# Cross-attention in fp32 on one core: seven products for three more batches, sums from ScalarE, roots from logarithms

## The chip, the core and the metric

The kernel runs on one core of a Trainium2 chip. A core has five engines that run side by side, each through its own queue in order: PE (TensorE, matmuls; its weight loads are shown apart as PEld), DVE (VectorE), ACT (ScalarE), POOL (GpSimd) and SP (SyncE, which issues DMAs here). They wait for each other through semaphores. The metric is the device time of the program in microseconds (us), the median of some runs.

## The reference

```python
Q = (img_embed @ Wq).reshape(B, -1, H, D).transpose(0, 2, 1, 3)
K = (sent_embed @ Wk).reshape(B, -1, H, D).transpose(0, 2, 1, 3)
V = (sent_embed @ Wv).reshape(B, -1, H, D).transpose(0, 2, 1, 3)
score = jnp.einsum('bhqd,bhkd->bhqk', Q, K) / math.sqrt(D)
score = jnp.where(mask, score, -jnp.inf)
attn = jax.nn.softmax(score, axis=-1)
ctx = jnp.einsum('bhqk,bhkd->bqhd', attn, V).reshape(B, -1, H * D)
out = ctx @ Wo + img_embed
mu = jnp.mean(out, axis=-1, keepdims=True)
var = jnp.var(out, axis=-1, keepdims=True)
return (out - mu) * jax.lax.rsqrt(var + EPS) * gamma + beta
```

There are 16 batches of 256 rows of `img_embed` (256 wide) and 77 rows of `sent_embed` (192 wide), 8 heads with D = 256. All is fp32.

## The kernel before

**Setup.** The weights are multiplied with each other first: `gA`, `gB` hold Wk and Wq of each head in one product, `uA`, `uB` hold Wv and Wo of each head in one product. A batch then needs three contractions: `a` (context times `gA`, `gB`), the scores `ps` (x times `a`), and the output `po` (softmax weights times `vw`, where `vw` is context times `uA`, `uB`).

**Tiles and groups.** A tile is 128 rows of x, so a batch has two tiles and there are 32. Four batches are a group: `xT` and `a` are made for a whole group ahead, one quarter in each batch of the group before. The last group (batches 12 to 15) has no group after it, so while its batches are scored PE has no `a` to make.

**The loop.** The order of the work is written out by hand in one loop over b from -1 to 14. A turn of the loop handles three batches at once: `new` are the tiles of batch b + 1 (scores, exponentials, weights), `now` those of batch b (output contraction), `old` those of batch b - 1 (layer norm, stored). Every engine takes its instructions in the order in which the turn names them:

- `scores` (PE, L311), `shift` (DVE: scores from PSUM plus the mask's bias, L326; the negated maximum of each head, L333);
- `prepare_vw` and `prepare_a` (PE, L239 and L250, L197 and L211); their results leave PSUM by copies on ACT (L884);
- `exponential` (ACT, L340, one instruction a head with that head's maximum as bias), `weigh` (DVE: the sum of each head over its 77 keys, L346, and its reciprocal, L348; POOL: the multiplication into `p`, two instructions at L354);
- `finish` (DVE: statistics of the layer norm, L482 and L485), `spread` (ACT: square root, L493), `invert` (DVE: reciprocal, L500), `normalise` (DVE: `centre`, L514, then L530; with `aside` ACT L524 and POOL L525, L526 instead, for which `invert` makes `less`, L504), then the store, a DMA that SP issues for each batch once both tiles are done;
- `turn` (DVE: transposes p in 32 x 32 blocks to `pT`, L364), `transpose_x` (DVE, L173, two in each of the last two batches of a group);
- for `now`, either `attend` or `seven`.

`attend` (L376) is the direct form: for each of the two tiles, five weight blocks against 256 columns. `seven` (L427) takes the two tiles, the two halves of the keys and the two halves of the columns as 2 x 2 blocks and forms them with seven block products instead of eight (the Strassen-Winograd scheme), plus the products of the last 13 keys. It needs the differences of `vw`'s parts (`differences`, POOL, L390, into `ts`), four sums of the weights (`sums`, POOL, L407 to L410, into `ss`), made a turn ahead, and after the products an ACT copy of four of them (`m`, L450) and `add_seven`: two additions of `po` on DVE (L474) and five additions on POOL (L460). `NS` is the number of batches that are done so: 11 before, batches 0 to 10. `prepare_vw` lays out `vw` for one form or the other.

**Tables.** ACT's functions come in sets of tables, of which one is loaded at a time. Exp and Sqrt stand in different ones in this program, so each turn loads two (the rows ACT_TABLE_LOAD at L493 and at L890 or L911). The tiny activation `warm` (L890, L911) makes the load for Exp happen before the exponentials are due.

**Buffers.** PSUM's eight banks are one ring, `ps_mm`: a new tile waits until the reader of the tile eight places before it is done. `s`, `e`, `p`, `ts`, `ss` are double buffered, `m` is single.

**The end.** After the loop the last batch is contracted with `attend`, and the last four tiles are finished and normalised one after the other, with DVE, ACT and POOL sharing the work.

Of the kernel before, what the change touches and what calls it, by code (L numbers as in the profile page):

```python
# [8 lines left out]
F32 = mybir.dt.float32  # L9
I32 = mybir.dt.int32  # L10
AF = mybir.ActivationFunctionType
# [4 lines left out]
P = 128  # L16
H = 8
# [36 lines left out]
def kernel(  # L54
# [53 lines left out]
    NH = DI // 2 // BK  # L108
    uA = const.tile([P, 5, NH, NF, BK], F32, tag="uA", name="uA")
    uB = const.tile([P, 5, NH, NF, BK], F32, tag="uB", name="uB")  # L110
    NS = B - GB - 1

    def of_e(u, e):
        return u[:, 3 - 2 * e : 5 - 2 * e].rearrange("p q n i c -> p (q n) i c")
# [218 lines left out]
        nc.vector.tensor_reduce(top, s, AX.X, ALU.max, negate=True)  # L333
        s_of[t] = s, top

    def exponential(t):
        e = sp.tile([P, H, S2], F32, tag="e", name=f"e_{t}")
        s, top = s_of.pop(t)
        for h in range(H):
            nc.scalar.activation(e[:, h], s[:, h], AF.Exp, bias=top[:, h : h + 1])  # L340
        e_of[t] = e

    def weigh(t):
        e = e_of.pop(t)
        den = st.tile([P, H], F32, tag="den", name=f"den_{t}")
        nc.vector.tensor_reduce(den, e, AX.X, ALU.add)  # L346
        rden = st.tile([P, H], F32, tag="rden", name=f"rden_{t}")
        nc.vector.reciprocal(rden, den)  # L348
        p = p_ring[t % 2]
        e_mh = e.rearrange("p (m h) k -> p m h k", h=2)  # L350
        rden_mh = rden.rearrange("p (m h) -> p m h", h=2)
        for cols, keys in ((slice(2 * KM), slice(KM)), (slice(2 * KM, 2 * S2), slice(KM, None))):
            part = p[:, :, cols].rearrange("p m (h k) -> p m h k", h=2)
            nc.gpsimd.tensor_tensor(  # L354
                part,
                e_mh[:, :, :, keys],
                rden_mh.unsqueeze(3).to_broadcast(list(part.shape)),
                ALU.mult,
            )

    def turn(t):
        p = p_ring[t % 2]
        pT_of[t] = turned.tile([P, NF + 1, NM, BK], F32, tag="pT", name=f"pT_{t}", bufs=4)
        nc.vector.transpose(  # L364
            pT_of[t].rearrange("p n m q -> p m n q"),
            p.rearrange("p m (n k) -> p m n k", k=BK),
        )
# [15 lines left out]
        po_of[t] = po  # L383


    def differences(b):

        vw = vw_of[b].rearrange("p q k d -> p q (k d)")
        ts = vwp.tile([P, 3, 2, P], F32, tag="ts", name=f"ts_{b}", bufs=2)
        nc.gpsimd.tensor_tensor(  # L390
            ts.rearrange("p q k d -> p q (k d)"),
            vw[:, 1:4],
            vw[:, 0:1].to_broadcast([P, 3, 2 * P]),
            ALU.subtract,
        )
        ts_of[b] = ts
# [16 lines left out]
    def seven(b):  # L413
        pT = [pT_of.pop(QT * b + i) for i in range(QT)]
        vw, ss = vw_of[b], ss_of.pop(b)
        ts = ts_of.pop(b)
        pm = ps_mm.tile([P, 4, P], F32, tag="mm", name=f"pm_{b}")
        po = ps_mm.tile([P, 4, P], F32, tag="mm", name=f"po_{b}")
        t2, b21, b22, b11 = (vw[:, q] for q in range(4))
        t4, t1, t3 = (ts[:, q] for q in range(3))  # L420
        s1, s3, s2, s4 = (ss[:, i] for i in range(4))
        ends = vr[:, b, :P], vr[:, b, P:]

        def contract(out, *terms):
            for n, (weight, moving) in enumerate(terms):
                for i in range(NM):
                    nc.tensor.matmul(  # L427
                        out[i * BK : (i + 1) * BK],
                        weight[:, i],
                        moving,  # L430
                        start=(n == 0),
                        stop=(n == len(terms) - 1),
                    )

        def block(weights, moving):
            return [(weights[:, k], moving[:, k]) for k in range(2)]

        last = [(pT[i][:, NF], vr[:, b, j * P : (j + 1) * P]) for i in range(QT) for j in range(2)]
        contract(pm[:, 0], *block(pT[0][:, 0:2], b11))
        contract(pm[:, 1], *block(s2, t2))  # L440
        contract(pm[:, 2], *block(s3, t3))
        contract(pm[:, 3], *block(s1, t1))
        contract(po[:, 0], *block(pT[0][:, 2:4], b21), last[0])
        contract(po[:, 1], *block(s4, b22), last[1])
        contract(po[:, 2], *block(pT[1][:, 2:4], t4), last[2])
        contract(po[:, 3], last[3])
        for i in range(QT):
            po_of[QT * b + i] = flat(po[:, 2 * i : 2 * i + 2])
        m = vwp.tile([P, 4, P], F32, tag="m", name=f"m_{b}", bufs=1)
        nc.scalar.copy(m, pm)  # L450
        m_of[b] = m
# [32 lines left out]
            mv_of[g] = st.tile([P, GT, 2], F32, tag="mv", name=f"mv_{g}", bufs=2)  # L484
        nc.vector.bn_aggr(mv_of[g][:, j, :], bn)  # L485

    std_of, rstd_of, done = {}, {}, []

    def spread(first, last):

        g, lo, hi = first // GT, first % GT, (last - 1) % GT + 1
        std = st.tile([P, GT], F32, tag="std", name=f"std_{first}")
        nc.scalar.activation(std[:, lo:hi], mv_of[g][:, lo:hi, 1], AF.Sqrt, bias=eps)  # L493
        std_of[first, last] = std

    def invert(first, last, aside=(), less_on=nc.gpsimd):

        g, lo, hi = first // GT, first % GT, (last - 1) % GT + 1
        rstd = st.tile([P, GT], F32, tag="rstd", name=f"rstd_{first}")
        nc.vector.reciprocal(rstd[:, lo:hi], std_of.pop((first, last))[:, lo:hi])  # L500
        if aside:
            less = st.tile([P, GT], F32, tag="less", name=f"less_{first}")
            for j in (t % GT for t in aside):
                less_on.tensor_scalar(  # L504
                    less[:, j : j + 1], mv_of[g][:, j, 0:1], rstd[:, j : j + 1], -1.0,
                    ALU.mult, ALU.mult,
                )
        for t in range(first, last):
            j = slice(t % GT, t % GT + 1)
            rstd_of[t] = rstd[:, j], less[:, j] if aside else None  # L510
# [33 lines left out]
    with tc.tile_pool(name="wonce", bufs=1) as wp:  # L544
# [49 lines left out]
            load_blocks(wk_blk[:, e], wk_blocks[2 * e + 1])  # L594
            load_blocks(wq_blk[:, e], wq_blocks[2 * e + 1])

        warm = const.tile([P, 1], F32, tag="warm", name="warm")
        nc.scalar.activation(warm, eps, AF.Exp)

        wvT = wp.tile([P, NF, NL, P], F32, tag="wvT", name="wvT")  # L600
        wo_of = [
# [252 lines left out]
    for b in range(-1, B - 1):  # L854
        old = range(max(b - 1, 0) * QT, b * QT)
        now = range(max(b, 0) * QT, (b + 1) * QT)
        new = range((b + 1) * QT, (b + 2) * QT)
        for t in new:
            scores(t)
        for t in new:  # L860
            shift(t)
        for n in range(0, 2) if b < 0 else range(b + 2, min(b + 3, B // 2)):
            turn_last(n)
        g, n = (b + 1) // GB + 1, (b + 1) % GB
        work = [prepare_vw(b + 1)]
        if g < NG:
            work.append(prepare_a(g, (n,)))
            if n == 0:
                load_xT(g)
                load_x(g)  # L870
        for part_A, _, _ in work:
            part_A()
        for _, part_B, _ in work:
            part_B()
        for i, t in enumerate(new):
            exponential(t)
            if old:
                finish(old[i])
            weigh(t)
        if old:  # L880
            spread(old[0], old[-1] + 1)
        for _, _, copies in work:
            for dst, src in copies():
                nc.scalar.copy(dst, src)  # L884
        if b + 1 < NS:
            differences(b + 1)
        if b < NS:
            if now:
                seven(b)
            nc.scalar.activation(warm, eps, AF.Exp)  # L890
            if old:
                invert(old[0], old[-1] + 1)
                normalise(old[0])
            for t in new:
                turn(t)
            if n >= NF - 2:
                for j in range((n - NF + 2) * GT // 2, (n - NF + 3) * GT // 2, 2):
                    transpose_x(g, j)
            if old:
                normalise(old[1])  # L900
            if now:
                add_seven(b)
            if b + 1 < NS:
                sums(b + 1)
            continue
        for t in now:
            attend(t)
        if b < B - 2:
            invert(old[0], old[-1] + 1, aside=old[:1])
            normalise(old[0], aside=True)  # L910
            nc.scalar.activation(warm, eps, AF.Exp)  # L911
            turn(new[0])
            normalise(old[1])
            turn(new[1])
            for t in now:
                add_product(t)
        else:
            turn(new[0])
            invert(old[0], old[-1] + 1, aside=old)
            for t in old:  # L920
                normalise(t, aside=True)
            turn(new[1])
            for t in now:
                finish(t)
            spread(now[0], now[-1] + 1)

# [48 lines left out]
```

## Time and profile before

| | |
|---|---|
| median of 3 runs | 278.14 us (277.98 to 279.79) |
| the profiled execution | 277.25 us, its span 275.5 us, granted clock 0.995 |
| busy: PE, PEld, DVE, ACT, POOL | 267.7, 192.2, 208.9, 165.4, 159.5 us |
| 256 exponentials (L340) | 67.2 us, mean 347 ns |
| 28 table loads (L493, L890, L911, L598) | 35.9 us, 1283 ns each |
| 32 sums of the softmax (L346) | 24.7 us, mean 772 ns |
| batches 0 to 10 in `seven` (L427) | 4.1 us of PE each |
| batches 11 to 15 in `attend` (L376) | 4.5 us of PE each |

The profile is of one execution, and its durations add up against that execution's own time. A line of a timeline gives start, duration, engine, line, operation, tiles and shapes, how many instructions are merged in it, and in brackets the idle time of the engine just before it with what ended it. Consecutive instructions of one engine can overlap by some tens of nanoseconds, so a row of them takes less than the sum of the durations. A line of the chain of waits gives start, length and what the program's end depended on there.

### The profile page before, as it was taken

To read this page: it belongs to the slowest core of one execution; us is meant where nothing else is said; L and a number is where in the kernel's file an instruction comes from. 1 tells how busy PE (TensorE), PEld (TensorE's weight loads), DVE (VectorE), ACT (ScalarE), POOL (GpSimd) and SP (SyncE) were. 2 spreads that over 40 slices of the span, in tenths; PEclk is the share of its full clock that TensorE was granted. 3 is DMA by queue.
4 is the path that set the end of the run, shared out by engine and by line. 5 is a ranking of instruction groups with operands and counts; after the bars stand their busy time and mean duration, and the time that the engine had idled before them with its cause. 6 is when DMAs were issued, how large, how long until landed. Compare 5 with 4: busy or idle time off the path is not lost.

```text
span 275.5 us, 13238 instructions
## 1 busy us (share of the span) xinstructions
PE 267.7 (97%) x5908; PEld 192.2 (70%) x5908; DVE 208.9 (76%) x423; ACT 165.4 (60%) x443; POOL 159.5 (58%) x221
## 2 busy tenths in 40 slices
PE   8999999999999999999999999999999999999991
PEld 7747487967494949496959595868686767575660
DVE  0453976877748989878788888777798887788885
ACT  3304112354819494958586767767685857869762
POOL 1000006919677777787877778777778436335184
PEclk9999999999999999999999999999999999999997
DMA  6996979980000102930101009501001010010103
GB/s 181 257 206 189 315 168 175 255 211 3 4 6 2 43 2 74 207 111 4 43 2 41 4 25 191 176 5 40 6 2 40 5 40 17 29 42 2 40 4 114
DMA packets 40201, 22.61 MB, mean 82 GB/s; under 512 B 23168, under 2 KB 38608, under 8 KB 40144
## 3 DMA queue, kind: packets, MB, share of 16 engines
q1 hardware_dynamic: 40000, 21.64, 31.8%
q8 instruction: 46, 0.75, 1.2%
q10 hardware_dynamic: 144, 0.13, 0.1%
q14 instruction: 11, 0.09, 0.1%
HBM read 17.57 MB, written 4.19 MB: 79 GB/s over the span
## 4 chain that ended last, share of the span: by engine, by line
PE 89%; DVE 4%; DMA 3%; ACT 2%; SPq 1%; POOL 1%; issue 0%; POOLq 0%; ACTq 0%
PE ps L311 24%; PE pa L197 12%; PE pv L239 9%; PE po L427 9%; PE pm L427 8%; PE pa L211 6%; PE pv L250 6%; PE po L376 5%; DMA c_sb<-in_ctx_dram 3%; PE pu L701 3%; PE pr L272 2%; ACT e L340 2%; PE pgb L701 1%; PE pw L715 1%; PE pr L282 1%; PE phb L715 1%
## 5 line engine op out<-in xcount | busy, mean ns | idle before, releaser
L340 ACT ACTIVATE e<-s,top 128x77 f32<-128x77 f32 x256 | 67.2, 347 | 52.0 <-DVE top L333 49.7
L354 POOL TENSOR_TENSOR p<-e,rden 128x512 f32<-128x512 f32 x64 | 45.8, 738 | 47.1 <-DVE rden L348 40.7
L311 PE MATMUL ps<-a,xT 128*32 128x154 f32 x2048 | 70.1, 294 | 0.0
L311 PEld LDWEIGHTS ps<-a,xT 128*32 128x32 f32 x2048 | 66.3, 110 | 1.7 <-issue 0.7
L326 DVE TENSOR_TENSOR s<-ps,bias 128x308 f32<-128x308 f32 x64 | 30.4, 475 | 17.6 <-PE ps L311 17.5
L197 PE MATMUL pa<-cA,gA 128*32 128x308 f32 x512 | 35.9, 423 | 0.0
L460 POOL TENSOR_TENSOR xg<-xg,m 128x256 f32<-128x256 f32 x33 | 24.2, 732 | 13.7 <-DVE xg L474 12.0
L197 PEld LDWEIGHTS pa<-cA,gA 128*32 128x32 f32 x512 | 17.2, 110 | 20.1 <-issue 7.7
L239 PE MATMUL pv<-uA,cA 128*32 128x512 f32 x256 | 30.5, 592 | 0.0
L364 DVE STREAM_TRANSPOSE pT<-p 128x640 f32<-128x640 f32 x32 | 25.6, 824 | 2.6 <-POOL p L354 2.6
L346 DVE TENSOR_REDUCE den<-e 128x8 f32<-128x616 f32 x32 | 24.7, 772 | 3.2 <-ACT e L340 3.2
L333 DVE TENSOR_REDUCE top<-s 128x8 f32<-128x616 f32 x32 | 25.4, 795 | 1.1
L390 POOL TENSOR_TENSOR ts<-vw 128x768 f32<-128x768 f32 x11 | 22.0, 1999 | 0.0
L211 PE MATMUL pa<-cB,gB 64*32 64x308 f32 x512 | 19.5, 420 | 0.0
L376 PE MATMUL po<-vw,pT 128*32 128x256 f32 x320 | 19.2, 380 | 0.0
L884 ACT COPY vw<-pv 128x512 f32<-128x512 f32 x32 | 16.9, 578 | 2.7 <-PE pv L250 2.7
L493 ACT ACT_TABLE_LOAD x14 | 18.0, 1283 | 0.3
L211 PEld LDWEIGHTS pa<-cB,gB 64*32 64x32 f32 x512 | 9.7, 107 | 11.3 <-issue 7.6
L250 PE MATMUL pv<-uB,cB 64*32 64x512 f32 x256 | 17.4, 601 | 0.0
L514 DVE SCALAR_TENSOR_TENSOR xg<-xg,mv,gam 128x256 f32<-128x256 f32 x25 | 17.2, 688 | 0.0
L376 PEld LDWEIGHTS po<-vw,pT 128*32 128x32 f32 x320 | 10.0, 110 | 9.5 <-DVE den L346 2.5
L884 ACT COPY a<-pa 128x308 f32<-128x308 f32 x48 | 16.6, 447 | 0.0
(118 smaller groups left out, 417.8 us busy)
## 6 DMA issues: line engine op xcount, KB each, us to landing
xT<-in_x_dram SPq DMA_DIRECT2D x16, 256.0 KB, 6.9
xg<-in_x_dram SPq DMA_DIRECT2D x4, 1024.0 KB, 7.9
out_dram<-xg SPq DMA_DIRECT2D x15, 256.0 KB, 2.1
wo<-in_L_xattn_Wo_dram SPq DMA_DIRECT2D x4, 512.0 KB, 5.6
wvT<-in_L_xattn_Wv_dram SPq DMA_DIRECT2D x16, 96.0 KB, 3.2
wq_nat<-in_L_xattn_Wq_dram SPq DMA_DIRECT2D x2, 512.0 KB, 6.0
wq_blk<-in_L_xattn_Wq_dram SPq DMA_DIRECT2D x8, 128.0 KB, 4.9
wk_blk<-in_L_xattn_Wk_dram SPq DMA_DIRECT2D x8, 96.0 KB, 5.5
```

Of the source, the lines that this page charges most:

```text
L197: nc.tensor.matmul(flat(o[i * BK : (i + 1) * BK]), gA[:, h, cols(dc, i)], flat(cA[:, batches, :]), start=not B_first, stop=B_first,)
L211: nc.tensor.matmul(flat(banks[j + k][i * BK : (i + 1) * BK]), gB[half(k), h % NF, cols(dc, i)], flat(cB[half(k), batches, :]), start=B_fir ...
L239: nc.tensor.matmul(pv[k][i * BK : (i + 1) * BK], cA[:, b, k * BK : (k + 1) * BK], uA[:, parts, :, i], start=True, stop=False,)
L250: nc.tensor.matmul(pv[k][i * BK : (i + 1) * BK], cB[half(k), b, k * BK : (k + 1) * BK], uB[half(k), parts, :, i], start=False, stop=True,)
L311: nc.tensor.matmul(ps[m // 2][i * BK : (i + 1) * BK, m % 2 * 2 * S2 : (m % 2 + 1) * 2 * S2], xT_of[g][:, j * NM + m, dc], flat(a_of[g][:, ...
L326: nc.vector.tensor_tensor(s[:, a * H // 2 : (a + 1) * H // 2], ps[a][:, : H // 2 * S2].rearrange("p (h k) -> p h k", k=S2), bias[:, b, :]. ...
L340: nc.scalar.activation(e[:, h], s[:, h], AF.Exp, bias=top[:, h : h + 1])
L354: nc.gpsimd.tensor_tensor(part, e_mh[:, :, :, keys], rden_mh.unsqueeze(3).to_broadcast(list(part.shape)), ALU.mult,)
L364: nc.vector.transpose(pT_of[t].rearrange("p n m q -> p m n q"), p.rearrange("p m (n k) -> p m n k", k=BK),)
L376: nc.tensor.matmul(po[i * BK : (i + 1) * BK], pT[:, n, i], vw_of[b][:, 2 - n // 2 * 2 : 4 - n // 2 * 2, n % 2, :] if n < NF else vr[:, b, ...
L427: nc.tensor.matmul(out[i * BK : (i + 1) * BK], weight[:, i], moving, start=(n == 0), stop=(n == len(terms) - 1),)
L884: nc.scalar.copy(dst, src)
```

## The change

- `NS` becomes B - 2 = 14: batches 11 to 13 also use `seven`. With that, `differences` and `sums` are made for batches 11 to 13 too; `differences` takes an engine as an argument, and it is POOL for batches up to 11, DVE for batches 12 and 13.
- In `seven` the products stand in another order: those that need only `pT`, `vw` and `ts` come first, those that need the sums of the weights later. This holds for all batches.
- The turns b = 11 to 13 have an order of their own: exponentials of the first new tile, statistics of the first old one, weights, statistics of the second old one, then the exponentials of the second new tile with `spread` between its fourth and fifth head; then `invert`, the first normalisation, the transpose of the first new tile, the weights of the second, the second normalisation; after the copies of `vw` the differences on DVE, `seven`, the second transpose, `add_seven`, `sums`. Both normalisations are on DVE there (one was aside on ACT and POOL).
- Each exponential gives the sum of its head as a second output (`accum_out`); the reduction at L346 goes.
- `spread` computes exp(-ln(var + eps) / 2) in two activations; `invert` loses its reciprocal. The set of tables that has both functions is loaded once at the start; the `warm` activations go.

```diff
-    NS = B - GB - 1
+    NS = B - 2
...
-    def exponential(t):
+    def exponential(t, between=None):
         e = sp.tile([P, H, S2], F32, tag="e", name=f"e_{t}")
+        den = st.tile([P, H], F32, tag="den", name=f"den_{t}")
         s, top = s_of.pop(t)
         for h in range(H):
-            nc.scalar.activation(e[:, h], s[:, h], AF.Exp, bias=top[:, h : h + 1])
-        e_of[t] = e
+            if between and h == H // 2:
+                between()
+            nc.scalar.activation(
+                e[:, h], s[:, h], AF.Exp, bias=top[:, h : h + 1], accum_out=den[:, h : h + 1]
+            )
+        e_of[t] = e, den
 
     def weigh(t):
-        e = e_of.pop(t)
-        den = st.tile([P, H], F32, tag="den", name=f"den_{t}")
-        nc.vector.tensor_reduce(den, e, AX.X, ALU.add)
+        e, den = e_of.pop(t)
...
-    def differences(b):
+    def differences(b, engine):
...
-        nc.gpsimd.tensor_tensor(
+        engine.tensor_tensor(
...
         contract(pm[:, 0], *block(pT[0][:, 0:2], b11))
+        contract(po[:, 0], *block(pT[0][:, 2:4], b21), last[0])
+        contract(po[:, 2], *block(pT[1][:, 2:4], t4), last[2])
         contract(pm[:, 1], *block(s2, t2))
         contract(pm[:, 2], *block(s3, t3))
         contract(pm[:, 3], *block(s1, t1))
-        contract(po[:, 0], *block(pT[0][:, 2:4], b21), last[0])
         contract(po[:, 1], *block(s4, b22), last[1])
-        contract(po[:, 2], *block(pT[1][:, 2:4], t4), last[2])
         contract(po[:, 3], last[3])
...
-        std = st.tile([P, GT], F32, tag="std", name=f"std_{first}")
-        nc.scalar.activation(std[:, lo:hi], mv_of[g][:, lo:hi, 1], AF.Sqrt, bias=eps)
-        std_of[first, last] = std
+        log = st.tile([P, GT], F32, tag="log", name=f"log_{first}")
+        rstd = st.tile([P, GT], F32, tag="rstd", name=f"rstd_{first}")
+        nc.scalar.activation(log[:, lo:hi], mv_of[g][:, lo:hi, 1], AF.Ln, bias=eps)
+        nc.scalar.activation(rstd[:, lo:hi], log[:, lo:hi], AF.Exp, scale=-0.5)
+        all_rstd_of[first, last] = rstd
...
-        rstd = st.tile([P, GT], F32, tag="rstd", name=f"rstd_{first}")
-        nc.vector.reciprocal(rstd[:, lo:hi], std_of.pop((first, last))[:, lo:hi])
+        rstd = all_rstd_of.pop((first, last))
...
-        warm = const.tile([P, 1], F32, tag="warm", name="warm")
-        nc.scalar.activation(warm, eps, AF.Exp)
+        nc.scalar.preload_act_table_set("natural_log_exp_and_others")
...
-        for i, t in enumerate(new):
-            exponential(t)
+        if g < NG or b == NS:
+            for i, t in enumerate(new):
+                exponential(t)
+                if old:
+                    finish(old[i])
+                weigh(t)
             if old:
-                finish(old[i])
-            weigh(t)
-        if old:
-            spread(old[0], old[-1] + 1)
+                spread(old[0], old[-1] + 1)
+        else:
+            exponential(new[0])
+            finish(old[0])
+            weigh(new[0])
+            finish(old[1])
+            exponential(new[1], between=lambda: spread(old[0], old[-1] + 1))
+            invert(old[0], old[-1] + 1)
+            normalise(old[0])
+            turn(new[0])
+            weigh(new[1])
+            normalise(old[1])
...
-        if b + 1 < NS:
-            differences(b + 1)
+        if g == NG and b < NS:
+            if b + 1 < NS:
+                differences(b + 1, nc.vector)
+            seven(b)
+            turn(new[1])
+            add_seven(b)
+            if b + 1 < NS:
+                sums(b + 1)
+            continue
         if b < NS:
+            differences(b + 1, nc.gpsimd)
...
-            nc.scalar.activation(warm, eps, AF.Exp)
...
-        if b < B - 2:
-            invert(old[0], old[-1] + 1, aside=old[:1])
-            normalise(old[0], aside=True)
-            nc.scalar.activation(warm, eps, AF.Exp)
-            turn(new[0])
-            normalise(old[1])
-            turn(new[1])
-            for t in now:
-                add_product(t)
```

More of the change, by code (lines that the diff above doesn't have):

```diff
@@ L485, in finish @@
         nc.vector.bn_aggr(mv_of[g][:, j, :], bn)
-    std_of, rstd_of, done = {}, {}, []
+    all_rstd_of, rstd_of, done = {}, {}, []
     def spread(first, last):
         g, lo, hi = first // GT, first % GT, (last - 1) % GT + 1
-        std = st.tile([P, GT], F32, tag="std", name=f"std_{first}")
-        nc.scalar.activation(std[:, lo:hi], mv_of[g][:, lo:hi, 1], AF.Sqrt, bias=eps)
-        std_of[first, last] = std
+        log = st.tile([P, GT], F32, tag="log", name=f"log_{first}")
[3 more added lines that the diff above has]
+        all_rstd_of[first, last] = rstd
     def invert(first, last, aside=(), less_on=nc.gpsimd):
-        g, lo, hi = first // GT, first % GT, (last - 1) % GT + 1
-        rstd = st.tile([P, GT], F32, tag="rstd", name=f"rstd_{first}")
-        nc.vector.reciprocal(rstd[:, lo:hi], std_of.pop((first, last))[:, lo:hi])
+        g = first // GT
+        rstd = all_rstd_of.pop((first, last))
         if aside:
@@ L902 @@
                 add_seven(b)
-            if b + 1 < NS:
-                sums(b + 1)
+            sums(b + 1)
             continue
@@ L907 @@
             attend(t)
-        if b < B - 2:
-            invert(old[0], old[-1] + 1, aside=old[:1])
-            normalise(old[0], aside=True)
-            nc.scalar.activation(warm, eps, AF.Exp)
-            turn(new[0])
-            normalise(old[1])
-            turn(new[1])
-            for t in now:
-                add_product(t)
[L917 to L925, printed above, removed]
+        turn(new[0])
+        invert(old[0], old[-1] + 1, aside=old)
+        for t in old:
+            normalise(t, aside=True)
+        turn(new[1])
+        for t in now:
+            finish(t)
+        spread(now[0], now[-1] + 1)
     for t in new:
```

## The prediction

> **What bounds the kernel now.** I read the busy shares first, then the chain that ended last, then each engine in order of time through one stage. The page's first part, then the pieces of the chain (start, us, what) around the hand-over from batch 10 to batch 11:
>
> ```profile
> PE 267.7 (97%) x5908; PEld 192.2 (70%) x5908; DVE 208.9 (76%) x423; ACT 165.4 (60%) x443; POOL 159.5 (58%) x221
> ```
> ```profile
> 215.81 1.88 PE pm L427 x64
> 217.69 2.18 PE po L427 x80
> 219.88 4.19 PE ps L311 x128
> 224.06 1.72 PE pv L239 x16
> 225.78 1.02 PE pv L250 x16
> 226.80 4.46 PE po L376 x80
> 231.25 4.19 PE ps L311 x128
> ```
>
> TensorE (PE) is never out of work from 11.5 us to the last scores at 256.15. A batch of groups 0 to 2 takes 14.10 us (205.59 to 219.69), one of the last group 11.38 (231.07 to 242.45). Seven products cost 1.88 + 2.18 = 4.06 us, the direct form of L376 costs 4.46. After 256.15 the chain leaves PE: scores, exponentials, weights, transpose, then VectorE (DVE) alone to the end.
>
> What the other engines have spare decides this change. First ScalarE (ACT), then DVE, in one batch of a middle group:
>
> ```profile
> 209.37 4.20 ACT L340 ACTIVATE e<-s,top 128x77 f32<-128x77 f32 x16 [3.52 <-DVE top L333]
> 213.58 1.28 ACT L493 ACT_TABLE_LOAD   x1
> 214.88 0.30 ACT L493 ACTIVATE std<-mv,eps 128x2 f32<-128x2 f32 x1
> ```
> ```profile
> 213.60 0.80 DVE L346 TENSOR_REDUCE den<-e 128x8 f32<-128x616 f32 x1 [0.28 <-ACT e L340]
> 214.43 0.20 DVE L348 RECIPROCAL rden<-den 128x8 f32<-128x8 f32 x1
> 215.21 0.17 DVE L500 RECIPROCAL rstd<-std 128x2 f32<-128x2 f32 x1 [0.58 <-ACT std L493]
> ...
> 220.99 0.48 DVE L326 TENSOR_TENSOR s<-ps,bias 128x308 f32<-128x308 f32 x1
> 222.04 0.48 DVE L326 TENSOR_TENSOR s<-ps,bias 128x308 f32<-128x308 f32 x1 [0.57 <-PE ps L311]
> ```
>
> Sixteen exponentials run in 4.20 us, one every 0.262. When the last ends (213.57), DVE still has 7.4 us of work in order before the next batch's scores, and arrives there (220.97) just as they do; only the 0.57 us wait on PE is spare. DVE and ACT thus form a second loop, scores to exponentials to DVE to scores, 0.57 us shorter than PE's.
>
> **What the Trainium skill says.** "ScalarE: Activation LUTs", section on what ACT_TABLE_LOAD costs: 1283 ns for the load, 186 ns + 0.833 ns an element for an ACTIVATE, some 93 more for a pointer operand, and neighbours overlap by some 93. The trace agrees: 28 loads of 1283; an exponential of 77 columns lasts 347 and follows at 262, an overlap of 85. The same page's section on table sets puts exp and ln in one set; no run here shows it yet. "VectorE: DVE Perf Modes", section on two Vector instructions with no wait between them, says that an operation that also writes out its accumulator is two instructions, the second a read without input. That is said of VectorE. No page prices it for ScalarE and the trace has no such row, so this is the one unknown that matters.
>
> **The change, part by part.**
>
> *Seven products for batches 11 to 13.* PE saves 4.46 - 4.06 = 0.40 us each, 1.2 us in all. The products in a new order, for all batches: the same instructions, nothing waits there now, so zero; what needs the four sums comes 1.3 us later (two products of 0.65), which only helps.
>
> *What the seven products need.* Pool, last group: four sums of 0.73 and five additions (2 x 0.48, 3 x 0.73) come, the moved-aside normalisation (0.48 + 0.73 + 0.73) goes: 4.67 + 6.1 - 1.9 = 8.9 us busy of 11.0. Batch 11's differences (2.0) and sums (2.9) go into batch 10's turn, where Pool idles 2.17 + 1.22 + 3.98. Cover enough; were it gone, PE would wait at the first product that reads a sum. ACT gains a copy of 0.59, loses one of 0.60. DVE: differences for batches 12 and 13 move to it (128x768, unseen there: between 0.95, extrapolated from 412 ns for 256 and 475 for 308, and 1.57, three times the 0.523 of L530; I take 1.0), and the second half of the normalisation (0.93). The output DMA of a batch is issued on SP after that; SP issues nothing else then.
>
> *Sums accumulated by ScalarE.* DVE loses two reductions of 0.80 a batch. Each of 256 exponentials gains a read, r. Lower end 0: it rides along. Upper end: a whole shortest ACTIVATE (the 0.204 of the warm-up) that overlaps nothing and spoils the next overlap too, 0.204 + 0.085 = 0.29. If it streams like any other it adds 0.204 - 0.085 = 0.12; if it must wait for its sum but the next overlaps it, 0.204. I take r = 0.15, between the last two, so 16 r = 2.4 us a batch.
>
> *Roots as exp(-ln/2).* Two loads and a warm-up leave each batch (2.8 us of ACT), one ACTIVATE of some 0.3 comes, and DVE loses the reciprocal (0.17) with its 0.58 wait. In the last group the pair stands in the middle of the second tile's exponentials: 0.55 more in front of the last. At the end of the kernel, rstd arrives as late as the DVE work beside it (L514's 0.67 hid the root and now hides ln and exp): about 0.15 saved over three stages.
>
> *Middle groups.* After its last exponential DVE now does 0.83 + 0.58 + 0.09 = 1.5 less (reduction, wait, reciprocal less its overlap). With the spare 0.57 the loop can take 2.07 us, r = 0.13, free. At r = 0.15 it misses by 0.33 in the two batches of a group that also transpose x (1.26 on DVE), and has 0.9 spare in the other two: PE isn't held, but 0.66 of lag enters the last group.
>
> *Last group.* The loop is 4.20 of exponentials, 0.55 for ln and exp, then DVE: rden 0.23, normalisation 0.86, differences 0.92, transpose 0.76, two additions 0.64, two scores and the maximum 1.75 (starts to starts at 241 to 248 us, PE waits taken out). That is 9.9, say 10.0 + 16 r, against PE's 10.98; the last of three rounds has no differences, 9.1. At r = 0.15: 2 x (12.4 - 10.98) + (11.5 - 10.98) = 3.4 us late.
>
> *End.* Both tiles' exponentials lie on the chain: + 2.4, less the reduction 0.83 and the 0.15: + 1.4.
>
> Sum: - 1.2 + 0.66 + 3.4 + 1.4 = + 4.3 us. Against the profiled execution (277.25; span 275.5 and 1.75 around it) that is 281.5. The median shown is 278.14, 0.9 above that execution, so on the scale of medians 282.4.
>
> **The rivals.** *The read streams or is free* (r up to 0.11): the other side, not slower. Decided at ScalarE by r = 0.06, from where the last group's loop exceeds PE's. Below it nothing is late: - 1.2 of PE and at most - 0.4 more, since the last two contractions then hold DVE at the end: 276.5. At r = 0.10: lag 2 x 0.6 + 0, end + 0.6, PE - 1.2: + 0.7, 278.8. For it: neighbours in the trace overlap, a read has no operand to fetch. *ACT and DVE become the bound everywhere* (r from 0.18): at 0.20 the middle groups miss 1.1 in two batches of four and recover almost nothing, up to 6 us in all; last group 2 x 2.2 + 1.3 = 5.7, end + 2.2, PE - 1.2: + 7 to + 13, 285 to 291. At 0.29 a middle batch misses 1.3 to 2.6: some + 33, 311. For it: a sum is complete only when its pass is. *The change buys nothing because DVE has no time in the last group* (differences at 1.57, contention with Pool): + 1.2 on any of these, inside the ranges.
>
> **How the numbers follow.** A measurement here tells about 1% (2.8 us) from no change. The forecast (r 0.12 to 0.17; 279.8 to 284.5) has 0.43, the free read 0.29, the bound everywhere 0.26, anything else 0.02. No case reaches 1% faster by its own arithmetic: 0.05 for what I don't see. Within 1% (up to 280.9, r to about 0.135): the free read and the lower third of the forecast, 0.35. Slower: 0.60. The range goes from 276.5 to 293, which leaves out the costly half of the third case.
>
> **What would show it.** Sixteen exponentials in 4.20 + 2.4 = 6.6 us; 0.204-like rows between them, or a longer row; one table load; no DVE den row; PE batches of 14.10 unchanged in the middle groups and 10.98 in the last; idle PE before the contraction of the second last tile, 2 to 4 us; the last scores end near 255, the last DVE instruction near 277. It is wrong if the sixteen take under 5.5 or over 7.2 us, or if PE idles in the middle groups.

## The result, and the profile after

The changed kernel takes 281.74 us, median of 4 runs (280.87 to 282.67), against 278.53 for the kernel before (277.98 to 279.79): 1.0122 times as long, interval 1.0093 to 1.0151. The forecast was 282.4. Much of the mechanism was not what it said, and most of this section is about that. The profiled execution took 281.92 us, its span 280.1, 4.6 more than before.

Part 1 of the page, busy shares of the kernel after:

```profile
PE 267.3 (95%) x6100; PEld 197.1 (70%) x6100; DVE 193.2 (69%) x382; ACT 151.2 (54%) x673; POOL 175.5 (63%) x240
```

DVE and ACT lost 15.7 and 14.2 us, PE 0.4, POOL gained 16, and the span is longer: the gains in busy time were nearly all in places that the end doesn't depend on.

**The read of the sum.** Part 5 of the page, groups of instructions (count, busy us, mean ns, idle before), and then ACT's timeline at the start of a middle batch's exponentials:

```profile
L343 ACT ACTIVATE e<-s,top 128x77 f32<-128x77 f32 x256 | 88.0, 346 | 62.8 <-DVE top L333 62.8
...
L343 ACT ACTIVATION_READ_ACCUMULATOR e<-s,top 128x1 f32 x256 | 47.9, 187 | 0.0
...
L534 DVE SCALAR_TENSOR_TENSOR xg<-xg,rstd,bet 128x256 f32<-128x256 f32 x28 | 23.8, 850 | 2.0 <-ACT rstd L498 0.2
```
```profile
198.68 0.36 ACT L343 ACTIVATE e<-s,top 128x77 f32<-128x77 f32 x1 [3.73 <-DVE top L333]
198.94 0.19 ACT L343 ACTIVATION_READ_ACCUMULATOR e<-s,top 128x1 f32 x1
199.03 0.34 ACT L343 ACTIVATE e<-s,top 128x77 f32<-128x77 f32 x1
```

The read is an instruction of its own, 187 ns long, and overlaps both neighbours: exponentials start 0.343 us apart. Sixteen with their reads go from 198.68 to the end of the last read, 204.08 + 0.19 = 204.27, 5.59 us instead of 4.20, so the read costs r = 0.09 each. The prediction took 0.15.

**The middle groups.** DVE's timeline between two batches there, and then in the last group:

```profile
204.30 0.20 DVE L351 RECIPROCAL rden<-den 128x8 f32<-128x8 f32 x1 [2.03 <-ACT e L343]
...
211.37 0.48 DVE L326 TENSOR_TENSOR s<-ps,bias 128x308 f32<-128x308 f32 x1 [0.46 <-PE ps L311]
...
231.55 0.48 DVE L534 SCALAR_TENSOR_TENSOR xg<-xg,rstd,bet 128x256 f32<-128x256 f32 x1 [0.18 <-ACT rstd L498]
...
233.51 1.16 DVE L534 SCALAR_TENSOR_TENSOR xg<-xg,rstd,bet 128x256 f32<-128x256 f32 x1
234.59 1.12 DVE L393 TENSOR_TENSOR ts<-vw 128x768 f32<-128x768 f32 x1
```

In the middle group DVE now waits 2.03 us for the sums and is back before PE's scores (the 0.46 is a wait for PE): the loop keeps up, batches are 14.10 us apart but for the two that the waits of PE below lengthen, and nothing is carried into the last group.

**The last group.** PE's batches there start at 223.13, 234.12, 245.11 and 256.10, 10.99 apart, but the exponentials at 226.88, 238.80, 250.73 and 261.97. The chain of waits from batch 10's output contraction on:

```profile
219.25 0.57 PE pm L430 x16
219.82 1.31 PE po L430 x48
221.13 1.31 PE pm L430 x48
222.44 0.87 PE po L430 x32
223.31 2.14 PE ps L311 x64
...
225.99 0.81 DVE top L333
...
231.52 1.38 ACT e L343 x8
232.90 0.02 issue
232.92 0.20 DVE rden L351
233.12 0.36 DVE xg L518
233.48 0.02 issue
233.51 1.16 DVE xg L534
234.66 1.04 DVE ts L393
235.71 0.75 DVE pT L367
236.46 0.64 DVE xg L477 x2
237.10 0.78 DVE s L326 x2
237.88 0.02 issue
237.91 0.81 DVE top L333
```

Before, this stretch of the chain lay on PE alone. Now it leaves PE at 225.45 and runs through ACT (226.88 to 232.92, 6.04 us) and DVE (232.92 to 238.80, 5.88 us): 11.92 a turn, 0.93 more than PE's batch. The row that stands out is L534 (the second instruction of `normalise`, L530 before), 1.16 us for what takes 0.48 a tile earlier (231.55). POOL at that time, from its timeline:

```profile
230.04 1.56 POOL L357 TENSOR_TENSOR p<-e,rden 128x512 f32<-128x512 f32 x2 [0.31 <-DVE rden L351]
233.20 1.69 POOL L357 TENSOR_TENSOR p<-e,rden 128x512 f32<-128x512 f32 x2 [1.60 <-DVE rden L351]
```

The 1.16 lies inside POOL's multiplication (233.20 to 234.89), the 0.48 falls just at the end of the one before (231.60). The Trainium skill, "SBUF — State Buffer", section "SBUF: two separate sides", says that a VectorE operation with two SBUF inputs and a GpSimd operation that reads SBUF take the same pair of ports as an exclusive lock, and that the later one waits. L534 has two such inputs (xg and beta). The trace agrees in kind: it costs DVE 0.68 us, and POOL's pair takes 1.69 here, 1.38 in the same place before the change (240.22 below), where DVE ran a transpose and reciprocals, with one input each. The other rows of the last group fit. The first instruction of `normalise`, L518, has two such inputs too; it takes 0.98 to 1.19 where POOL's multiplication is already under way (230.39, 242.31, 254.24), 0.43 where it starts ahead of it (233.04, 244.97, 256.90). No run moves the multiplication alone, so that it is the cause is read from these rows, not from an experiment. The kernel before shows the same in its middle groups, where L514 took 0.82 at 215.29, inside POOL's pair, and 0.44 at 241.49, just at the end of one:

```profile
214.78 1.56 POOL L354 TENSOR_TENSOR p<-e,rden 128x512 f32<-128x512 f32 x2 [0.45 <-DVE rden L348]
240.22 1.38 POOL L354 TENSOR_TENSOR p<-e,rden 128x512 f32<-128x512 f32 x2 [0.42 <-DVE rden L348]
```
```profile
215.29 0.82 DVE L514 SCALAR_TENSOR_TENSOR xg<-xg,mv,gam 128x256 f32<-128x256 f32 x1
241.49 0.44 DVE L514 SCALAR_TENSOR_TENSOR xg<-xg,mv,gam 128x256 f32<-128x256 f32 x1
```

**Waits of PE.** From the view of waits after 60 us; before the change that view is empty for PE:

```profile
PE po L430 <- issue: 2.2, 1, 2.2
PE po L379 <- DVE pT L367: 1.0, 1, 1.0
```

The second is the lag arriving at the last contractions. The first the prediction doesn't have at all. PE's timeline around it:

```profile
120.57 0.27 PE L430 MATMUL po<-vw,ss 128*32 128x128 f32 x1
123.02 0.53 PE L430 MATMUL po<-vw,ss 128*32 128x128 f32 x12 [2.18 <-issue]
```

It stops after the first instruction of a block of sixteen, whose operands that instruction already reads, so no semaphore holds it. The view of DMA by queue for two windows, 112.5 to 120.3 us, then 120.3 to 123.1 (packets, MB, share of 16 engines):

```profile
q1 hardware_dynamic: 3448, 1.61, 123.2%
q14 instruction: 1, 0.01, 0.3%
```
```profile
q1 hardware_dynamic: 321, 0.32, 33.8%
q8 instruction: 1, 0.02, 2.5%
```

Queue 8 carries instructions, 48 packets of 16,384 bytes in the whole program (46 before); the count follows PE's matmuls and weight loads, 12,200 (11,816), one packet for some 256 of them. Packets mostly come every 3 to 8 us. Here one ended at 112.4 and the next came at 120.46, with the transfers of the next group's x in between (2 MB: four of xT, the x of the scores, at 256 KB and one of xg, the x to which the output is added, at 1 MB, issued together at the first turn of a group). PE ran on what it had, stopped at 120.84, and went on 1.5 us after the packet had landed. In the kernel before, the packet came at 117.8 in the same place, in time.

**Where the profiled 4.6 us went:** 0.6 ahead of the first scores, which start at 54.24 before and at 54.85 after; 2.8 between them and the scores of batch 12, the first of the last group (165.45 us before, 168.28 after), of which 2.18 are that wait and 0.5 fall on the batch from 180.32 to 194.93, 14.61 long; 1.2 from there to the end (55.8 us before, 57.0 after): - 1.2 of PE, + 2.1 of lag, + 0.2 at the end (15.22 to 15.37 from the last batch's exponentials to the last DVE instruction).

### The profile page after: what moved, and what is told of

Same layout as the page of the kernel before. It is cut to its first block, busy times and chain, and to the rows that moved or that the text cites. A ratio compares the mean times of both kernels' runs of the same rounds, so it can differ in the third digit from the quotient of the medians.

```text
span 280.1 us, 13822 instructions
## 1 busy us (share of the span) xinstructions
PE 267.3 (95%) x6100; PEld 197.1 (70%) x6100; DVE 193.2 (69%) x382; ACT 151.2 (54%) x673; POOL 175.5 (63%) x240
## 4 chain that ended last, share of the span: by engine, by line
PE 75%; DVE 10%; ACT 6%; DMA 3%; issue 2%; POOL 1%; SPq 1%; ACTq 0%; DVEq 0%
PE ps L311 19%; PE pa L197 12%; PE po L430 9%; PE pv L239 7%; PE pm L430 7%; PE pa L211 6%; ACT e L343 6%; PE pv L250 4%; DMA c_sb<-in_ctx_dram 3%; PE pu L704 3%; PE pr L272 2%; DVE pT L367 2%; DVE xg L534 1%; PE pgb L704 1%; DVE xg L518 1%
## 5 line engine op out<-in xcount | busy, mean ns | idle before, releaser
L343 ACT ACTIVATE e<-s,top 128x77 f32<-128x77 f32 x256 | 88.0, 346 | 62.8 <-DVE top L333 62.8
L357 POOL TENSOR_TENSOR p<-e,rden 128x512 f32<-128x512 f32 x64 | 48.7, 781 | 36.5 <-DVE rden L351 36.5
L343 ACT ACTIVATION_READ_ACCUMULATOR e<-s,top 128x1 f32 x256 | 47.9, 187 | 0.0
L326 DVE TENSOR_TENSOR s<-ps,bias 128x308 f32<-128x308 f32 x64 | 29.4, 471 | 12.2 <-PE ps L311 12.2
L463 POOL TENSOR_TENSOR xg<-xg,m 128x256 f32<-128x256 f32 x42 | 30.8, 733 | 5.8 <-DVE xg L477 3.0
L351 DVE RECIPROCAL rden<-den 128x8 f32<-128x8 f32 x32 | 6.3, 198 | 31.8 <-ACT e L343 31.6
L534 DVE SCALAR_TENSOR_TENSOR xg<-xg,rstd,bet 128x256 f32<-128x256 f32 x28 | 23.8, 850 | 2.0 <-ACT rstd L498 0.2
L463 POOL TENSOR_TENSOR m<-m 128x128 f32<-128x128 f32 x28 | 14.6, 521 | 12.9 <-ACT m L453 11.8
L430 PE MATMUL po<-vr,pT 128*32 128x128 f32 x448 | 20.1, 273 | 0.0
L453 ACT COPY m<-pm 128x512 f32<-128x512 f32 x14 | 8.2, 585 | 17.2 <-PE pm L430 17.2
```

The lines of the kernel that those rows point to most:

```text
L326: nc.vector.tensor_tensor(s[:, a * H // 2 : (a + 1) * H // 2], ps[a][:, : H // 2 * S2].rearrange("p (h k) -> p h k", k=S2), bias[:, b, :]. ...
L357: nc.gpsimd.tensor_tensor(part, e_mh[:, :, :, keys], rden_mh.unsqueeze(3).to_broadcast(list(part.shape)), ALU.mult,)
L430: nc.tensor.matmul(out[i * BK : (i + 1) * BK], weight[:, i], moving, start=(n == 0), stop=(n == len(terms) - 1),)
L463: nc.gpsimd.tensor_tensor(to, to, what, ALU.add)
L534: nc.vector.scalar_tensor_tensor(y, y, rstd, bet, ALU.mult, ALU.add)
```

## The experiments

**First set: the change taken apart.** In the expectations S is the theory that the time is lost in the last group, where seven products shorten PE's batch and ACT and DVE do not follow, and in waits of PE for instructions; R is the rival, that the reads cost wherever they stand. The kernel before took 277.97 us there.

*Sums from ScalarE alone*, on the kernel before:

```diff
-            nc.scalar.activation(e[:, h], s[:, h], AF.Exp, bias=top[:, h : h + 1])
+            nc.scalar.activation(
+                e[:, h], s[:, h], AF.Exp, bias=top[:, h : h + 1], accum_out=den[:, h : h + 1]
+            )
...
-        nc.vector.tensor_reduce(den, e, AX.X, ALU.add)
```

> The kernel before with the sums from ScalarE alone (accum_out, no reduction at L346); tables, roots and the last group as before. Theory S (the loss sits in the last group's ScalarE-VectorE loop and in PE waiting for instructions, not in the reads of the middle groups): sixteen exponentials take 5.5 us instead of 4.2, middle batches stay at 14.10, the end gets 1.3 - 0.8 = 0.5 longer: 278.5 to 279.2. Theory R (the 256 reads cost time all along): 280.5 to 281.5.

Measured: 282.25 us, 1.0148 (1.0114 to 1.0181), above both. Its waits of PE after 60 us:

```profile
PE po L377 <- ACT vw L885: 2.4, 1, 2.4
PE po L428 <- issue: 1.8, 1, 1.8
```

With the table loads still in every turn, reads and loads together lengthen the loop to 12.12 us in the last group, where PE's batch is 11.37; from batch 12's scores to the end is 2.7 longer than before. The rest is the second line: the same wait for instructions as in the whole change, at the same place, and here PE's program is the same as before, 5908 matmuls. S names such waits, but its range left no room for either part.

*Roots from logarithms alone*, on the kernel before:

```diff
-        nc.scalar.activation(std[:, lo:hi], mv_of[g][:, lo:hi, 1], AF.Sqrt, bias=eps)
...
+        nc.scalar.activation(log[:, lo:hi], mv_of[g][:, lo:hi, 1], AF.Ln, bias=eps)
+        nc.scalar.activation(rstd[:, lo:hi], log[:, lo:hi], AF.Exp, scale=-0.5)
...
-        nc.vector.reciprocal(rstd[:, lo:hi], std_of.pop((first, last))[:, lo:hi])
...
-        nc.scalar.activation(warm, eps, AF.Exp)
+        nc.scalar.preload_act_table_set("natural_log_exp_and_others")
```

> The kernel before with the roots as exp(-ln/2) and one table load, nothing else. Both theories: ScalarE is freed of 2.8 us a batch that nobody waited for; 0.1 to 0.2 less at the end: 278.2 to 278.6. If it is clearly faster, table loads were on the path after all.

Measured: 279.96 us, 1.007 (1.0029 to 1.0111): a miss. From batch 12's scores to the end it is 0.4 shorter, 55.4 for 55.8, where 0.1 to 0.2 was expected, but PE stops twice, with nothing to wait for. PE's timeline:

```profile
61.67 1.48 PE L239 MATMUL pv<-uA,cA 128*32 128x512 f32 x10 [1.87 <-issue]
...
124.38 0.53 PE L427 MATMUL po<-ts,pT 128*32 128x128 f32 x12 [0.92 <-issue]
```

Both stand beside a transfer of a group's x. An edit that only takes work from ACT and DVE gives PE nothing new to wait for, unless what holds it is its supply of instructions. A count of the traces' rows bears this out. The stop at 120 to 124 us comes after the same number of PE's instructions, 2,261 matmuls and as many weight loads, in the whole change and in all four kernels of this set, whichever product stands there. The first stop here comes after 729 matmuls, and a second one of sums with roots (below) after 3,794. These lie 1,532 and 1,533 matmuls from it, with their weight loads some twelve packets of 256.

*The whole change without the sums* (the reductions on DVE again):

```diff
-            nc.scalar.activation(
-                e[:, h], s[:, h], AF.Exp, bias=top[:, h : h + 1], accum_out=den[:, h : h + 1]
-            )
+            nc.scalar.activation(e[:, h], s[:, h], AF.Exp, bias=top[:, h : h + 1])
...
+        nc.vector.tensor_reduce(den, e, AX.X, ALU.add)
```

> The changed kernel with the sums back on VectorE (reduction as before, no accum_out). Theory S: the sixteen exponentials of a batch return to 4.2 us, VectorE does two reductions of 0.8 more; the last group's loop changes by - 1.3 + 0.8 a batch, the end by - 1.3 + 0.8; what the seven products put into the loop stays: 280 to 281.5. Theory R: all of the loss goes, 278.5 or less.

Measured: 282.84 us, 1.0185 (1.0155 to 1.0215), above S's range too; 1.08 us of it is PE waiting on issue at 122.82. R falls: taking the reads away doesn't help. The seven products need room on DVE more than on ACT.

*Sums and roots without the seven products* (both edits above on the kernel before, so no diff of its own):

> The kernel before with the sums from ScalarE and the roots as exp(-ln/2), batches 11 to 13 in the direct form and in the old order. Theory S: no lag in the last group, + 0.3 at the end: 278.4 to 279. Theory R: 280.5 to 281.5.

Measured: 280.54 us, 1.0088 (1.0056 to 1.012), as R has it, but not for R's reason: from batch 12's scores to the end it takes as long as the kernel before (55.85), and PE waits for instructions instead, 1.87 + 0.36 us.

**Second set: the supply of instructions.** The 2 MB of x are spread over the four turns of a group instead of one; nothing else is changed:

```diff
-            if n == 0:
-                load_xT(g)
-                load_x(g)
+            if n < 2:
+                load_xT(g, (2 * n, 2 * n + 1))
+            else:
+                load_x(g, (n - 2,))
```

Four kernels had it: the kernel before, the changed one, the roots alone, and sums with roots. The kernel before as it was took 278.71 there.

> The kernel before, with a group's 2 MB of x no longer loaded in one burst in the group's first turn but a quarter in each of its four turns. Theory F (TensorE's own instructions, fetched as 16 KB packets, queue behind that burst; the wait of 1 to 2 us near 122 us and its like make up what the last group does not explain): no TensorE wait on issue in the middle groups; 276 to 277.5 if the kernel before pays a little of it too. Rival P (the parts of the change slow every batch a little, the burst is innocent): 278, as before.

> The changed kernel with x loaded in quarters. Theory F: the kernel before with quarters plus 1.2 us (last group + 2.1, end + 0.2, TensorE - 1.2): 277.2 to 278.7. Rival P: still 3.2 us over the kernel before with quarters, 281 to 281.7.

> Roots as exp(-ln/2) and one table load alone, with x in quarters. Theory F: the kernel before with quarters less 0.4 us, from the end: 275.6 to 277.1. Rival P: 2 us over the kernel before with quarters.

> Sums from ScalarE and the roots, no seven products in the last group, x in quarters. Theory F: equal to the kernel before with quarters within 0.3 us. Rival P: 2.5 us over it.

| | x at once: us, ratio | x in quarters: us, ratio (interval) |
|---|---|---|
| before | 278.71, 1 | 278.03, 0.9972 (0.9957 to 0.9988) |
| roots alone | 279.96, 1.007 | 278.11, 0.9978 (0.9957 to 1.0) |
| sums and roots | 280.54, 1.0088 | 278.86, 0.9994 (0.9972 to 1.0015) |
| all of it | 281.74, 1.0122 | 280.55, 1.0065 (1.0043 to 1.0087) |

Ratios are each to the kernel before on the same chip. None of the four profiles has a wait of PE on issue after 60 us, and the middle batches are 14.10 apart. Against the kernel before in the same layout of x, the cost of the roots falls from 2.0 us to 0.1 and that of sums and roots from 2.6 to 0.8. So this wait was nearly all the cost of the roots and most of that of sums and roots, which speaks against P. The times do not all fall where F put them: the kernel before with x in quarters is P's number, the roots show nothing of their shorter end in the median, and the 0.8 us left of sums and roots, where at most 0.3 was expected, is not in its one profile (span 276.1 against 276.4) and stays open. The kernel before gains 0.28% by the quarters, so it had a little of that wait; with its x in quarters it is, beside the roots with x in quarters, the best of all kernels here that compute everything.

The quarters make the wait rarer, not impossible: two kernels of the third set, the one without differences and the one with the old order of products, idle on issue for 0.4 and 0.7 us before 60.53 and 61.29, after the same 729 matmuls as the roots' first stop.

The whole change keeps 2.5 us over its like, where 1.2 had been expected; its time lies between the two theories' ranges. With x at once (four runs) the difference was 3.2, so in the timed runs the quarters take 0.7 us of the cost away, less than the wait's 2.2 in the profile. The traces show 1.1 of the 2.5 in the last group and the end (57.2 against 56.1), and the time around the span is 0.34 longer (2.13 against 1.79, medians of 20). About 1.1 is left. In the one profile of it the first scores start 1.5 us later than in its like (56.41 against 54.87), after waits of PE for a weight's transfer in the setup. With x at once the same kernel starts them at 54.85. Whether they start late in every run, and what the change has to do with it, wasn't shown.

**Third set: the last group.** All four are the changed kernel with x in quarters, 280.55 us; the kernel before took 278.56 there. D is the theory that the lag comes from the loop of ACT and DVE in the last group, G the rival, that GpSimd, 10 of 11.9 us busy there, is what binds. The changed kernel's exponentials, with the starts of two turns:

```profile
225.46 0.36 ACT L346 ACTIVATE e<-s,top 128x77 f32<-128x77 f32 x1 [3.73 <-DVE top L336]
...
237.38 0.36 ACT L346 ACTIVATE e<-s,top 128x77 f32<-128x77 f32 x1 [4.48 <-DVE top L336]
```

*Without the differences of batches 12 and 13* (the kernel leaves them out and uses batch 11's again, so it does less work than the task asks):

```diff
...
     def differences(b, engine):
+        if b >= B - GB:
+            ts_of[b] = kept[-1]
+            return
...
```

> The changed kernel with x in quarters (280.55), the differences for batches 12 and 13 left out (batch 11's are used again). Theory D (the last group's loop runs over ScalarE and VectorE, every VectorE instruction after the last exponential counts in full): two of the three turns lose 1.0 us and fall to TensorE's 10.99; the lag of 2.1 shrinks to about 0.3: 278.5 to 279. Rival G (GpSimd, 10 of 11.9 us busy, is what binds): no change beyond 0.5, 280 to 280.6.

Measured: 277.95 us, 0.9987 (0.9967 to 1.0008), below D's range: a gain of 2.6 us, where D had at most 2. The same view:

```profile
225.38 0.36 ACT L346 ACTIVATE e<-s,top 128x77 f32<-128x77 f32 x1 [3.73 <-DVE top L336]
...
236.61 0.36 ACT L346 ACTIVATE e<-s,top 128x77 f32<-128x77 f32 x1 [3.79 <-DVE top L336]
```

The turn falls from 11.92 to 11.23, still 0.24 above PE's, and the transpose then waits 0.26 for POOL's multiplication, which the differences had hidden. From batch 12's scores to the end the trace is 1.4 shorter (55.8 against 57.2); the rest of the gain lies elsewhere.

*Without the reads in batches 12 to 15* (the kernel leaves the sums out there; an exponential stands in for each):

```diff
+            if t < (B - GB) * QT:
                 nc.scalar.activation(
                     e[:, h], s[:, h], AF.Exp, bias=top[:, h : h + 1], accum_out=den[:, h : h + 1]
                 )
+            else:
+                nc.scalar.activation(e[:, h], s[:, h], AF.Exp, bias=top[:, h : h + 1])
...
-        nc.vector.reciprocal(rden, den)
+        nc.vector.reciprocal(rden, den if t < (B - GB) * QT else e[:, :, 0])
```

> The changed kernel with x in quarters (280.55), batches 12 to 15 without the sums (no accum_out; the first exponential of each head stands in for its sum). Theory D: the loop's turns lose 16 x 0.08 = 1.3 us and fall to TensorE's 10.99, the lag of 2.1 goes, the end loses 1.3 more: 277 to 277.5, which is below the kernel before with quarters (278.03). Rival G: only the end's 1.3: 279.2.

Measured: 277.47 us, 0.9956 (0.9934 to 0.9977). D's range, but the turns don't fall to PE's: the exponentials start at 224.07, 235.35, 247.11 and 258.19, 11.28, 11.76 and 11.08 apart, so half of the lag of 2.1 is left. Some 1.5 us of the gain come from the end (13.90 from the last exponentials to the last DVE instruction, against 15.36). From 225.2 to 240.2 us DVE has no wait in this kernel: without reads, DVE's own work, with POOL's interference in it, fills the turn.

*Without the sums*, the same edit as in the first set, on x in quarters:

> The changed kernel with x in quarters and the sums back on VectorE everywhere. Theory D: in the last group and at the end together 1.7 us longer than with the sums on ScalarE (two reductions of 0.8 a batch for sixteen reads of 0.08): 281.5 to 282.5. Rival R (the reads are what costs): below 280.5.

Measured: 281.91 us, 1.0112 (1.0077 to 1.0148); the trace from batch 12's scores to the end is 1.8 longer than with the sums. Waits of PE:

```profile
PE po L381 <- DVE pT L369: 1.5, 1, 1.5
...
PE pm L432 <- POOL ss L414: 0.9, 1, 0.9
```

*With the products in the old order:*

```diff
-        contract(po[:, 0], *block(pT[0][:, 2:4], b21), last[0])
-        contract(po[:, 2], *block(pT[1][:, 2:4], t4), last[2])
         contract(pm[:, 1], *block(s2, t2))
...
+        contract(po[:, 0], *block(pT[0][:, 2:4], b21), last[0])
         contract(po[:, 1], *block(s4, b22), last[1])
+        contract(po[:, 2], *block(pT[1][:, 2:4], t4), last[2])
```

> The changed kernel with x in quarters, the seven products in the old order for all batches. Theory D: middle groups as they are; in the last group TensorE meets the sums 1.3 us earlier and waits some 0.6 us a turn for GpSimd, off the chain: 280.5 to 281.2.

Measured: 281.6 us, 1.0105 (1.0073 to 1.0138), more than expected. PE then does wait for the weights' sums:

```profile
PE pm L433 <- POOL ss L415: 0.6, 1, 0.6
```

But PE is ahead of the exponentials by then, and from batch 12's scores to the end the trace takes 57.1 us, for 57.2 with the new order. The intervals of the two kernels overlap. That the order is worth the 1.05 us between the medians isn't shown.

## Why the prediction was right, and where it was not

The direction was right, and of the four terms the first. The time, 282.4 for 281.74, came out of steps whose errors cancelled: that it is so close is luck. The sum was - 1.2 + 0.66 + 3.4 + 1.4 = + 4.3. The trace has - 1.2 + 0 + 2.1 + 0.2 = + 1.1 (1.2 unrounded) for these four, and 3.4 that no step named.

- **Sums, "I take r = 0.15".** Measured 0.09, under even the value it gave for a read that streams (0.12). By its own cases the outcome is the rival "streams or is free", which it gave 0.29 and 278.8 us at r = 0.10. This is the size whose error went into most terms: sixteen take 5.6 us where it said 6.6. The overlap of 85 ns that it read is a mean over sixteen; in a row the exponentials before start 0.25 us apart (209.37, 209.63, 209.88), an overlap of some 0.10, and with that its streaming read would have cost 0.204 - 0.10 = 0.10.
- **Middle groups, "0.66 of lag enters the last group".** None does. The method held: 2.07 us free against 1.4 used. Only r was off.
- **Last group, "10.0 + 16 r".** With r = 0.09 that is 11.4; the trace has 11.92, then 11.24 for the round without differences, where 9.1 + 1.4 = 10.5 was forecast. The ACT part was right to 0.1 (4.20 + 1.4 + 0.55 = 6.15, measured 6.04). The DVE part was 5.16 and is 5.88: the reciprocal and the normalisation 0.65 more, by POOL's multiplication beside it, the differences 0.12. (The low end of 0.95 for the differences isn't what its two points give: a straight line through 412 ns for 256 columns and 475 for 308 comes to 1.03 for 768, and 1.04 from start to start was measured.) In the last round 0.26 more is a wait for POOL. The durations were taken from the stretch from 241 to 248 us of the trace before, where the normalisation met only the last 0.1 us of POOL's multiplication; the middle groups of that trace, where it did, would have shown the longer one. Contention stood as a third rival, priced at + 1.2 and put "inside the ranges"; it is why the lag is 2.1 and not the 2 x (11.4 - 10.98) = 0.8 or less that r alone would have left.
- **PE, "0.40 us each, 1.2 us in all".** Right: 10.99 a batch for 10.98. The idle time before the contraction of the second last tile is 1.0, for 2 to 4 forecast.
- **End, "+ 1.4".** + 0.2. The two tiles' reads cost 1.4 there by r, and the reduction and the roots give back more than forecast: roots alone shorten the end by 0.4, not 0.15.
- **Roots and tables.** One load, no other cost: right. That Exp and Ln share a set, as the Trainium skill says in "ScalarE: Activation LUTs", section on table sets, is shown by the single load of the trace.
- **Product order at zero.** The trace with the old order agrees from batch 12 on; the timed runs don't decide it.
- **What no step had.** "It is wrong if PE idles in the middle groups": it does, for 2.18 us at 120.84. The prediction took PE's instructions as given. Moving the loads of x took the cost of roots alone from 2.0 us to 0.1, so the wait is shown as a cause there; of the whole change's cost it took 0.7 of 3.2. Why the transfers took longer in the changed kernel than in the kernel before (xT 7.8 us to landing for 6.9, xg 9.2 for 7.9), and in roots alone (7.4 and 8.5), isn't known; roots alone make the same transfers, and PE's program there is that of before. In the profile of the changed kernel this wait is 2.2 of the 4.6 us.

The direction is right for the changed kernel in either layout of x: with quarters it is slower than its like by 0.9% (2.5 us). That work of DVE and ACT in the last group and at the end costs time is shown by the two kernels that leave some of it out: without the differences the time is 277.95, without the last reads 277.47, about that of the kernel before with x in quarters, 278.03. Neither shows a gain that is there to be had, since each does less than the task asks. Of the 2.5 us the traces place 1.1 in the last group and the end and 0.34 around the span; about 1.1 stays open.

## What to carry to other kernels

A shorter bottleneck pays only until the next loop's length, here ACT and DVE in turn; add that loop up with durations measured beside the same neighbours, because an operation with two inputs from SBUF cost 0.48 us alone and 1.16 beside POOL. When the busiest engine stops with nothing to wait for, look for its instruction packets in the DMA queues: here a burst of loads held them up, and spreading the burst over the time at hand cost nothing. A total that comes out right proves no term of its sum; compare the terms.

## What was not expected of the hardware

- PE's instructions come by DMA in packets of 16,384 bytes, some 256 instructions each (12,200 for 48 packets), and come late beside other transfers: with 2 MB of loads issued together PE idled up to 2.2 us; with the same loads in quarters, in two of eight profiles, 0.7 us at most. The stop near 121 us fell after the same 2,261 matmuls in five kernels.
- The read of ScalarE's accumulator is a row of its own, 187 ns, but adds only 0.09 us to each of a row of exponentials of 77 columns.
- An fp32 VectorE operation of 128 x 256 with two inputs from SBUF took 0.48 us alone and 1.16 when it started inside a GpSimd multiplication; the 128 x 768 subtraction took 1.12 on VectorE and 1.84 (mean of twelve) on GpSimd.
